# Convolution over f of the first batch: the mean is subtracted on VectorE and the constant goes into the gelu

## The chip, the cores and the metric

The kernel runs on one core of one Trainium2 chip. Its metric is the device time of one execution in microseconds (us), lower is better. Before the change the median of three runs is 3683.86 us, with 3683.42 and 3687.7 us as the lowest and the highest.

## The reference, cut to what matters

Two layers run one after the other on x of shape (4, 512, 128, 64), all in float32: four batches b, 512 time steps t, and 128 x 64 = 8192 features d = (f, h). The first layer is the one that is changed:

```python
xn = layernorm(x.reshape(b, t, d), ln_attn_g, ln_attn_b)
k, v, r = xn @ Wk, xn @ Wv, sigmoid(xn @ Wr)
states = scan over t of  s = decay * s + k * v
x = x + (r * states) @ Wo
xn = layernorm(x.reshape(b, t, d), ln_freq_g, ln_freq_b)   # statistics over all 8192 features
fo = conv over f, 3 taps, 64 x 64 channels h, of xn         # 'SAME' padding
x = x + gelu(fo + freq_b)
x = x + layernorm(causal depthwise conv over t, 3 taps, of layernorm(x))
x = x + W2 gelu(W1 x + b1) + b2                             # over h, 64 -> 256 -> 64
```

The second layer is a moving average over t plus a filter in the Fourier domain. It comes after the whole first layer and is not touched.

With rs = 1/sqrt(var + eps) and m the mean of one time step, the normalized value is x1\*rs - m\*rs. Each of these is one value per time step, so a row of 512 numbers that is the same for all features.

## The kernel before

The features lie on the partitions: a batch is 64 chunks of 128 features (two values of f, 64 of h) by 512 time steps, and the work goes in 32 pairs of chunks. A pair is a tile of 128 x 1024 float32. Each float32 matmul of the code stands in the trace as two matmul records.

For each batch b the first layer is made of stages, written as Python generators:

- `project` (J): k, v and r for all 512 steps, summed over the 32 pairs on TensorE (L412), with the weights scaled on VectorE (L359) and the statistics of the layernorm.
- `scan` (Z): the recurrence on VectorE with a few matmuls, which ends in rows for the next norm.
- `attend_and_convolve` (A): for each pair i, `attend(i)` makes x1 = x + Wo product (TensorE L534, VectorE L538) and z = x1 \* rs (VectorE L542). `convolve(i)` makes the convolution over f of pair i in PSUM, the gelu in place in PSUM (ScalarE L574), x2 = gelu + x1 (VectorE L576), the store of x2 (POOL queue, L579) and its square (ScalarE L581). `add_up` sums x2 and its square over the features with matmuls by ones (L250). The steps are staggered: step i attends pair i, convolves pair i-2 and adds up pair i-3.
- `convolve_time` (C), `open_feed` and `feed_forward` (O, F): the causal convolution over t and the feed forward.

The convolution leaves out the mean in z, and brings it in by a product of small rank. For every pair `convolve` has three groups of matmuls into the same PSUM tile `cv`: four 64 x 64 products of two constant rows of weights `cgs` with two rows `mb` (L560; one row is m\*rs, the other is ones, so that the mean and the constant from ln_freq_b and freq_b come in together); four 64 x 64 products with the neighbouring values of f (L568); and two full 128 x 128 products of the chunks themselves (L573). The constant rows are made once in `prepare`, written to DRAM (`cgd`), and read back two rows at a time: `scaled(i+2)` issues two small transfers from the SP queue (L548) and scales the taps on ScalarE (L553). Line L524 turns half of the rows of `mb` into ones.

TensorE's order is written out by hand: `in_turn` draws steps from two streams of stages by weights. For the first batch the streams are Z and A of batch 0 beside J and Z of batch 1, and after that C of batch 0 beside A of batch 1. The other engines' order comes from the scheduler. While J of batch 1 runs, its sums hold the PSUM tile `m` (`held`), so that every convolution of batch 0 uses the one tile `c`. Later the pairs take turns between `m` and `c`.

The pools matter too: the input tile `xp` has three buffers that J and A share, the weights `wk` of J have two, `cgs` three, `z` four.

Of the kernel before, what the change touches and what calls it, by code (L numbers as in the profile page):

```python
# [10 lines left out]
F32 = mybir.dt.float32  # L11
AF = mybir.ActivationFunctionType
ALU = mybir.AluOpType
# [3 lines left out]
P = 128  # L17
# [4 lines left out]
NCH = D // P  # L22
SL = 512
NS = D // SL
NPR = NCH // 2
# [55 lines left out]
def layer0(ctx, tc, dram, x, xt, vecs, wkvr, wo, wdec, wconv, fbias, w1, fb1, w2, fb2, x4):  # L81
# [4 lines left out]
    nc = tc.nc  # L86
# [9 lines left out]
    const = ctx.enter_context(tc.tile_pool(name="const", bufs=1))  # L96
# [9 lines left out]
    def two(pool, tag):  # L106
        return pool.tile([P, 2, SL], F32, tag=tag, name=tag)
# [47 lines left out]
    at_one = const.tile([P, 2], F32, name="at_one")  # L155
    nc.vector.tensor_reduce(at_one[:, 0:1], ident.rearrange("p (q k) -> p q k", k=32)[:, :, 1], mybir.AxisListType.X, ALU.add)
    nc.vector.tensor_scalar(at_one[:, 1:2], at_one[:, 0:1], -1.0, 1.0, ALU.mult, ALU.add)
    tb_all = vec[:, TB, :]
    fix = vec[:, G3 : B3 + 1, :].rearrange("p k c -> p c k")

    AHEAD = 14
    halves = [slice(0, H), slice(H, P)]

    def neighbours(q, c):

        return (c - 1, q), (c + 1, 1 - q)

    def rows_of(q, d):

        return 1 - q if d < 0 else q  # L170

    def prepare():

        both = rowp.tile([P, SL], F32, tag="rg", name="both")[:, 0:P].rearrange("p (k c) -> p k c", k=2)

        pcs = two(ps_c, "c"), two(ps_m, "m")
        for k, v in ((0, G2), (1, B2)):
            for r in range(2):
                for q in range(2):
                    j = r if q == 0 else 1 - r  # L180
                    o, src = pcs[r][:, k, 0:NCH], vec[:, v, :]
                    at = slice(2 * q + j, NCH, 4)
                    nc.tensor.matmul(
                        o[:, at], lhsT=wc_sb[:, q, 0:P], rhs=src[:, at], start=q == 0, stop=True,
                        skip_group_check=True,
                    )
                for q in range(2):
                    j = r if q == 0 else 1 - r
                    for d, n in neighbours(q, 0):
                        first, last = 2 * q + j, 2 * q + j + NCH - 4  # L190
                        first, last = first + 4 * (first + d < 0), last - 4 * (last + d >= NCH)
                        qn = (first + d) // 2 % 2
                        rs = halves[rows_of(qn, d)]
                        nc.tensor.matmul(
                            pcs[r][halves[n], k, first : last + 1 : 4], lhsT=wc_sb[rs, qn, P:],
                            rhs=vec[rs, v, first + d : last + d + 1 : 4], start=False, stop=True,
                            skip_group_check=True,
                        )
        for r in range(2):
            for q in range(2):  # L200
                at = slice(2 * q + (r if q == 0 else 1 - r), NCH, 4)
                nc.vector.tensor_scalar_mul(both[:, 0, at], pcs[r][:, 0, at], -1.0)
                nc.vector.tensor_scalar(both[:, 1, at], pcs[r][:, 1, at], fb_sb, None, ALU.add)
        pg = two(ps_c, "c")
        nc.tensor.transpose(pg[:, 0, 0:P], both.rearrange("p k c -> p (k c)"), ident)
        cgt = rowp.tile([P, SL], F32, tag="state", name="cgt")[:, 0:P]
        nc.vector.tensor_copy(cgt, pg[:, 0, 0:P])
        for k in range(2):
            nc.scalar.dma_start(cgd[:, k, :], cgt[k * NCH : (k + 1) * NCH, :])

        t012 = rowp.tile([P, SL], F32, tag="rg", name="t012")[:, 0 : 3 * NCH].rearrange("p (k c) -> p k c", k=3)
        t0, t1, t2 = t012[:, 0, :], t012[:, 1, :], t012[:, 2, :]
        nc.vector.tensor_tensor(t0, vec[:, W0, :], vec[:, B3, :], ALU.mult)
        nc.vector.tensor_tensor(t1, vec[:, W1, :], vec[:, B3, :], ALU.mult)
        nc.vector.tensor_tensor(t1, t1, t0, ALU.add)
        nc.vector.tensor_tensor(t2, vec[:, W2, :], vec[:, B3, :], ALU.mult)
        nc.vector.tensor_tensor(t2, t2, t1, ALU.add)
        nc.vector.tensor_tensor(tb_all, vec[:, TB, :], t2, ALU.add)  # L220
        for k in (W0, W1, W2):
            nc.vector.tensor_tensor(vec[:, k, :], vec[:, k, :], vec[:, G3, :], ALU.mult)
        nc.vector.tensor_scalar_mul(fix[:, :, 0], t1, -1.0)
        nc.vector.tensor_scalar_mul(fix[:, :, 1], t0, -1.0)
# [63 lines left out]
    def pair_of(row):  # L288
        return row.unsqueeze(1).to_broadcast([P, 2, SL])
# [11 lines left out]
    def c_bank():  # L301
        return two(ps_c, "c")
# [217 lines left out]
    def attend_and_convolve(b):  # L520
        rst, rs, mrs = scanned.pop(b)
        rb, mb = yield from rows(of_a, rs, mrs, "rm4" if b == 1 else "rm")

        nc.vector.tensor_scalar(mb, mb, at_one[:, 1:2], at_one[:, 0:1], ALU.mult, ALU.add)  # L524
        x1s, zs, ws, waiting = {}, {}, {}, {}

        def attend(i):
            xp = load_x(b, i)
            wo_sb = fr.tile([P, P], F32, tag="wo", name="wo_sb")
            nc.sync.dma_start(wo_sb, wo[:, i, :])  # L530
            at = two(ps_a, "a")
            for j in range(2):
                for hs in halves:
                    nc.tensor.matmul(  # L534
                        at[hs, j, :], lhsT=wo_sb[halves[j], hs], rhs=rst[halves[j], :], start=True, stop=True
                    )
            x1 = x1s[i] = fr.tile([P, 2, SL], F32, tag="x1", name="x1")
            nc.vector.tensor_tensor(x1, at, xp, ALU.add)  # L538
            z = fr.tile([P, 2, SL], F32, tag="z", name="z", bufs=4)
            for j in range(2):  # L540
                zs[2 * i + j] = z[:, j, :]
            nc.vector.tensor_tensor(z, x1, pair_of(rb), ALU.mult)  # L542

        def scaled(i):

            for j in range(2):
                at = H * (j ^ i % 2)
                nc.sync.dma_start(cgs[i % 3][at : at + 2, :], cgd[2 * i + j])  # L548
            wcs = fr.tile([P, 2, P + H], F32, tag="wcs", name="wcs")
            for j in range(2):  # L550
                c = 2 * i + j
                ws[c] = wcs[:, j, :]
                nc.scalar.mul(wcs[:, j, :], wc_sb[:, i % 2, :], vec[:, G2, c : c + 1])  # L553

        def convolve(i):
            cv = c_bank() if i % 2 or held[0] else two(ps_m, "m")
            for j in range(2):
                rs = halves[j ^ i % 2]
                for hs in halves:
                    nc.tensor.matmul(  # L560
                        cv[hs, j, :], lhsT=cgs[i % 3][rs, hs], rhs=mb[rs, :], start=True, stop=False
                    )
            for j in range(2):
                c = 2 * i + j
                for n, h in neighbours(i % 2, c):
                    if 0 <= n < NCH:
                        rs = halves[rows_of(n // 2 % 2, n - c)]
                        nc.tensor.matmul(  # L568
                            cv[halves[h], j, :], lhsT=ws[n][rs, P:], rhs=zs[n][rs, :], start=False, stop=False
                        )  # L570
            for j in range(2):
                c = 2 * i + j
                nc.tensor.matmul(cv[:, j, :], lhsT=ws[c][:, 0:P], rhs=zs[c], start=False, stop=True)  # L573
            nc.scalar.activation(cv, cv, AF.Gelu_apprx_tanh)  # L574
            x2 = two(bk, "x2")
            whole_x2 = nc.vector.tensor_tensor(x2, cv, x1s.pop(i), ALU.add)  # L576
            if i == NPR - 2:
                begin[project] = whole_x2.ins
            nc.gpsimd.dma_start(x2d[b][2 * i : 2 * i + 2].rearrange("c p t -> p c t"), x2)  # L579
            sq2 = bk.tile([P, 2, SL], F32, tag="sq", name="sq2")  # L580
            nc.scalar.activation(sq2, x2, AF.Square)  # L581
            for c in (2 * i - 2, 2 * i - 1):
                zs.pop(c, None)
                ws.pop(c, None)
            if i + 2 < NPR:
                scaled(i + 2)
            waiting[i] = x2, sq2
# [282 lines left out]
    def nothing(b):  # L870
# [5 lines left out]
    whole = {  # L876
        J: 2.0 * NPR, Z: 7 * CHAIN, A: 7.0 * NPR + 3 * CHAIN, C: 7.0 * (NPR + 2) + 3 * CHAIN, O: 4 * CHAIN,
        F: 9.0 * (NPR + 1), nothing: 1.0,
    }
# [345 lines left out]
```

## Time and profile before

| | us |
|---|---|
| median of three runs | 3683.86 |
| the profiled execution, its own time | 3685.27 |
| span of the profiled execution | 3683.5 |
| TensorE busy in the span | 3480.4 (94%) |
| VectorE busy | 2671.6 (73%) |
| ScalarE busy | 1778.1 (48%) |
| GpSimd busy | 448.4 (12%) |
| mean granted TensorE clock | 0.985 of full |

The profiled execution is 1.8 us longer than its span. Busy time of TensorE counts a matmul from its start to the modelled end, and several small matmuls in different parts of the array run at once, so 94% does not mean that the array is at its peak. What the change touches is `attend_and_convolve` of batch 0 only, whose first convolution starts at 242 us and whose last gelu starts at 515 us of the span. The stages of the other batches are not changed.

### The profile page before, as it was taken

Reading aid. Unit: us, or ns where it says so; the run is one execution under the profiler, and the core shown is the slowest. Engines: PE = TensorE matmul, PEld = TensorE weight load, DVE = VectorE, ACT = ScalarE, POOL = GpSimd, SP = SyncE. Lnnn points to the kernel's source line nnn. Section 1 sums busy time; section 2 is a strip of 40 time slices with the busy share of each in tenths; the row PEclk is TensorE's granted clock in tenths of the full one; section 3 lists DMA queues with packets and bytes.
Section 4 is the critical chain, followed back from the end, with each engine's and each line's share of the span. In section 5 each row is a group of like instructions: output and inputs, shape, how many; then the busy total and the mean of one; then the engine's idle time right before and its main releaser. Section 6 shows DMA issues by size and latency. Waiting matters only on the chain. (4 is left out here: it accounts for less than half of the span.)

```text
span 3683.5 us, 54528 instructions
## 1 busy us (share of the span) xinstructions
PE 3480.4 (94%) x20553; PEld 1372.7 (37%) x20553; DVE 2671.6 (73%) x3498; ACT 1778.1 (48%) x2331; POOL 448.4 (12%) x657
## 2 busy tenths in 40 slices
PE   8989998889999899999999989999999999999998
PEld 3433332224333223443322333333333833328433
DVE  4464469986777896677789799956677277892677
ACT  0013346556666565666656588878864200152100
POOL 0000012220111121011112121200000000001000
PEclk9999999999999999999999999999999999999999
DMA  9886647787885688888568777746668478994687
GB/s 302 284 269 211 204 164 269 255 277 264 294 288 183 237 279 280 277 289 292 172 239 284 239 238 256 238 173 218 225 194 277 154 245 293 308 290 161 209 298 261
DMA packets 427991, 910.58 MB, mean 247 GB/s; under 512 B 32976, under 2 KB 83920, under 8 KB 423632
## 3 DMA queue, kind: packets, MB, share of 16 engines
q1 hardware_dynamic: 354160, 637.18, 53.1%
q0 software_dynamic: 71680, 268.46, 20.3%
q8 instruction: 164, 2.69, 0.3%
q10 hardware_dynamic: 1888, 1.45, 0.1%
q14 instruction: 99, 0.81, 0.1%
HBM read 638.46 MB, written 268.50 MB: 246 GB/s over the span
## 5 line engine op out<-in xcount | busy, mean ns | idle before, releaser
L760 PE MATMUL p<-mid,w_sb 64*64 64x512 f32 x2048 | 549.3, 595 | 17.9 <-DVE wx L773 17.9
L760 PE MATMUL pb<-mid,w_sb 64*64 64x512 f32 x2048 | 533.2, 595 | 0.0
L750 ACT ACTIVATE mid<-m,fb_sb 128x1024 f32<-128x1024 f32 x256 | 284.8, 1113 | 93.0 <-PE m L745 91.6
L750 ACT ACTIVATE mid<-c,fb_sb 128x1024 f32<-128x1024 f32 x256 | 284.5, 1111 | 91.2 <-PE c L745 89.1
L745 PE MATMUL m<-x,w_sb 64*64 64x512 f32 x2016 | 283.3, 613 | 7.5 <-ACT ob L794 5.3
L745 PE MATMUL c<-x,w_sb 64*64 64x512 f32 x2016 | 276.9, 604 | 12.9 <-ACT mid L750 6.6
L760 PEld LDWEIGHTS p<-mid,w_sb 64*64 64x64 f32 x2048 | 153.7, 134 | 290.9 <-issue 261.0
L1071 ACT COPY two<-a 128x512 f32<-128x512 f32 x64 | 37.5, 586 | 426.3 <-PE a L1066 426.3
L412 PE MATMUL a<-xp,wx 128*128 128x512 f32 x512 | 235.2, 603 | 0.5 <-DVE me L267 0.5
L1094 PE MATMUL b<-xin,avg_sb 128*128 128x512 f32 x512 | 230.8, 593 | 3.3 <-DVE xin L1100 3.3
L1100 DVE TENSOR_TENSOR xin<-b,pm 128x512 f32<-128x512 f32 x256 | 159.0, 683 | 97.9 <-PE b L1097 82.9
L581 ACT ACTIVATE sq<-x 128x1024 f32<-128x1024 f32 x128 | 135.1, 1055 | 150.5 <-DVE x L576 150.4
L250 PE MATMUL st<-x,ones 128*32 128x512 f32 x512 | 183.9, 609 | 23.8 <-DVE x L576 23.7
L636 DVE SCALAR_TENSOR_TENSOR to<-kd,vec,to 128x511 f32<-128x511 f32 (+1 forms) x272 | 197.0, 743 | 11.5 <-ACT to L632 8.0
L713 ACT ACTIVATE kd<-kd,vec 128x512 f32<-128x512 f32 x256 | 192.7, 803 | 3.1 <-DVE kd L705 3.1
L538 DVE TENSOR_TENSOR x<-a,xp 128x1024 f32<-128x1024 f32 x128 | 156.1, 1219 | 48.1 <-PE a L534 45.5
L946 DVE COPY xf<-b 128x256 f32<-128x256 f32 x128 | 54.4, 425 | 178.9 <-PE b L1040 170.0
L636 DVE SCALAR_TENSOR_TENSOR z<-x,vec,z 128x511 f32<-128x511 f32 x240 | 175.6, 744 | 5.0 <-ACT z L632 3.6
L716 DVE TENSOR_TENSOR x<-kd,kx 128x1024 f32<-128x1024 f32 x126 | 154.0, 1223 | 33.5 <-ACT kd L713 33.5
L534 PE MATMUL a<-rst,wo_sb 64*64 64x512 f32 x1024 | 143.3, 630 | 27.4 <-DVE x L538 25.3
L773 DVE SCALAR_TENSOR_TENSOR x4t<-p,fb_sb,x 128x512 f32<-128x512 f32 x64 | 47.7, 746 | 160.0 <-PE pb L760 157.5
L704 DVE TENSOR_TENSOR kd<-kh,rm 128x1024 f32<-128x1024 f32 x128 | 155.6, 1219 | 6.8 <-ACT rm L284 4.6
(271 smaller groups left out, 6762.7 us busy)
## 6 DMA issues: line engine op xcount, KB each, us to landing
xp<-in_xt SPq DMA_DIRECT2D x256, 512.0 KB
kh<-to SPq DMA_DIRECT2D x156, 512.0 KB
x<-x POOLq DMA_DIRECT2D x128, 512.0 KB, 4.6
kx<-x SPq DMA_DIRECT2D x128, 512.0 KB
x<-ob POOLq DMA_DIRECT2D x64, 1024.0 KB, 8.1
xin<-x SPq DMA_DIRECT2D x64, 1024.0 KB
out<-xin POOLq DMA_DIRECT2D x64, 1024.0 KB, 6.3
x<-x SPq DMA_DIRECT2D x96, 512.0 KB
```

The costliest lines, as they stand in the source:

```text
L250: nc.tensor.matmul(st[32 * q : 32 * q + 32, :], lhsT=ones, rhs=src[:, j, :], start=first, stop=last,)
L412: nc.tensor.matmul(pa[:, k, :], lhsT=wq[:, j, k * P : (k + 1) * P], rhs=xp[:, j, :], start=first and j == 0, stop=last and j == 1,)
L538: nc.vector.tensor_tensor(x1, at, xp, ALU.add)
L636: tap = nc.vector.scalar_tensor_tensor(to[:, j, k:], xr[:, j, : SL - k], vec[:, w, c], to[:, j, k:], ALU.mult, ALU.add)
L704: nc.vector.tensor_tensor(d, to, pair_of(rb), ALU.mult)
L713: tc.keep_in_program_order(nc.scalar.activation(d[:, j, :], d[:, j, :], AF.Identity, bias=vec[:, B4, c], scale=vec[:, G4, c]))
L716: nc.vector.tensor_tensor(x3, d, x2, ALU.add)
L745: nc.tensor.matmul(pm[halves[j], h, :], lhsT=w1_sb[halves[h], q * H : (q + 1) * H], rhs=x3[halves[h], j, :], start=True, stop=True,)
L750: gelu = nc.scalar.activation(mid, pm, AF.Gelu_apprx_tanh, bias=fb1_sb[:, q : q + 1])
L760: nc.tensor.matmul(sums2[i][j][halves[h], :], lhsT=w2_sb[halves[j], q, :], rhs=mid[halves[j], h, :], start=q == 0, stop=q == 3,)
L1094: nc.tensor.matmul(po[j], lhsT=avg_sb[:, j, :], rhs=xin[:, j, :], start=True, stop=False)
L1100: nc.vector.tensor_tensor(by_n(xin[:, j, :]), by_n(po[j]), by_c(pm[j % 2][:, j // 2, :]), ALU.add)
```

## The change

For batch 0 alone (`whole`), the mean is subtracted from z on VectorE right after the product with rs, the four products with constant rows are left out together with the transfers of their weights, and the constant (a column of 128 values for each chunk, `cbias`, kept when `prepare` makes it) is the bias of the gelu. As the bias differs from chunk to chunk, the gelu becomes two instructions of 128 x 512 in place of one of 128 x 1024. As no product covers the whole tile any more before the neighbours' products, these start the sums themselves, with the chunk's own products after them; at the two ends, where a neighbour is missing, the own products come first. Line L524 is left out for batch 0.

```diff
@@ layer0, prepare
+    cbias = const.tile([P, NCH], F32, name="cbias")
...
+        nc.vector.tensor_copy(cbias, both[:, 1, :])
@@ attend_and_convolve
-        nc.vector.tensor_scalar(mb, mb, at_one[:, 1:2], at_one[:, 0:1], ALU.mult, ALU.add)
+        whole = b == 0
+        if not whole:
+            nc.vector.tensor_scalar(mb, mb, at_one[:, 1:2], at_one[:, 0:1], ALU.mult, ALU.add)
@@ attend
             nc.vector.tensor_tensor(z, x1, pair_of(rb), ALU.mult)
+            if whole:
+                nc.vector.tensor_tensor(z, z, pair_of(mb), ALU.subtract)
@@ scaled
-            for j in range(2):
+            for j in range(2 * (not whole)):
                 at = H * (j ^ i % 2)
                 nc.sync.dma_start(cgs[i % 3][at : at + 2, :], cgd[2 * i + j])
@@ convolve
-            for j in range(2):
+            for j in range(2 * (not whole)):
                 rs = halves[j ^ i % 2]
                 for hs in halves:
                     nc.tensor.matmul(
                         cv[hs, j, :], lhsT=cgs[i % 3][rs, hs], rhs=mb[rs, :], start=True, stop=False
                     )
+
+            def own(start):
+                for j in range(2):
+                    c = 2 * i + j
+                    nc.tensor.matmul(cv[:, j, :], lhsT=ws[c][:, 0:P], rhs=zs[c], start=start, stop=True, skip_group_check=whole)
+
+            edge = whole and i in (0, NPR - 1)
+            if edge:
+                own(True)
...
                         nc.tensor.matmul(
-                            cv[halves[h], j, :], lhsT=ws[n][rs, P:], rhs=zs[n][rs, :], start=False, stop=False
+                            cv[halves[h], j, :], lhsT=ws[n][rs, P:], rhs=zs[n][rs, :],
+                            start=whole and not edge, stop=whole, skip_group_check=whole,
                         )
-            for j in range(2):
-                c = 2 * i + j
-                nc.tensor.matmul(cv[:, j, :], lhsT=ws[c][:, 0:P], rhs=zs[c], start=False, stop=True)
-            nc.scalar.activation(cv, cv, AF.Gelu_apprx_tanh)
+            if not edge:
+                own(False)
+            if whole:
+                for j in range(2):
+                    c = slice(2 * i + j, 2 * i + j + 1)
+                    nc.scalar.activation(cv[:, j, :], cv[:, j, :], AF.Gelu_apprx_tanh, bias=cbias[:, c])
+            else:
+                nc.scalar.activation(cv, cv, AF.Gelu_apprx_tanh)
```

## The prediction, made before the changed kernel ran

> **What bounds the kernel now.** I read the busy times by stage first, then TensorE's order of time inside one pair, then what VectorE waits for, then the end of the stage.
>
> ```profile
> core 0: us, PE busy (x) PEld busy (x) DVE busy (x) ACT busy (x) POOL busy (x), PEclk, DMA share, GB/s
> 250.00:450.00 200.00, 199.88 (x976) 66.46 (x972) 95.61 (x116) 65.12 (x90) 18.25 (x25) 1.00 0.64 214
> 450.00:475.00 25.00, 24.31 (x142) 8.71 (x134) 17.38 (x20) 13.89 (x20) 2.18 (x3) 1.00 0.58 195
> 475.00:500.00 25.00, 21.73 (x114) 9.05 (x114) 11.62 (x16) 6.89 (x10) 2.79 (x4) 0.80 0.37 129
> 500.00:520.00 20.00, 18.94 (x112) 5.05 (x114) 9.39 (x9) 10.94 (x17) 3.01 (x4) 1.00 0.36 131
> 545.00:800.00 255.00, 226.29 (x1273) 58.94 (x1271) 252.66 (x280) 157.02 (x215) 68.86 (x92) 0.99 0.78 261
> ```
>
> The convolutions of batch 0 lie between 242 and 515 us. From 250 to 450 us, beside `project` of batch 1, TensorE is never idle, VectorE and ScalarE are under half, the transfers at 0.64. From 545 us on (C of batch 0 with A of batch 1) VectorE is the bound, 252.66 of 255. So time won before 545 us moves everything behind it forward; no later stage waits for a fixed moment.
>
> ```profile
> 447.91 0.21 PEld L534 LDWEIGHTS a<-rst,wo_sb 64*64 64x64 f32 x8 [0.84 <-issue]
> 448.39 0.15 PEld L560 LDWEIGHTS c<-rm,cg 64*64 64x64 f32 x4 [0.28 <-issue]
> 448.82 0.15 PEld L560 LDWEIGHTS c<-rm,cg 64*64 64x64 f32 x4 [0.28 <-issue]
> 449.25 0.15 PEld L568 LDWEIGHTS c<-z,wcs 64*64 64x64 f32 x4 [0.28 <-issue]
> 450.64 0.30 PEld L573 LDWEIGHTS c<-z,wcs 128*128 128x128 f32 x2 [0.81 <-issue]
> ```
>
> The mean duration must not be summed here: eight records of L560 at 589 ns would be 4.7 us a pair. The starts show the truth: four run at once, the two sets of four start 0.43 us apart, and L568 follows at 449.25. The constant products hold TensorE for 449.25 - 448.39 = 0.86 us a pair.
>
> The gelu begins at 272.90 in the fourth pair and at 436.22 in the 22nd: 163.32 us for 18 pairs, 9.07 us a pair. TensorE's sets make up 8.57 of that at 0.43 us each: 8 for L412, 4 for L573, and 2 for each of L250, L534, L560 and L568. The rest is the gaps between kinds of tile. So the pair is bound by TensorE's issue.
>
> **The change, part by part.**
>
> *The constant products go.* 20 pairs (the fourth to the 23rd) x 0.855 = 17.1 us on the path, if nothing else takes the place. The order listings of both kernels agree on TensorE apart from these 128 products and the ends' own products.
>
> *The subtraction comes.* 32 x 1.22 us, by the equal operation of `convolve_time` (L627, 128x1024, mean 1216 ns), 39 us in all on VectorE. In the steady stage it has a cover: VectorE is busy 95.61 of 200, and 20 more subtractions make 120 of some 183. z is first read by the convolution one step later. What stands behind it in VectorE's queue is one of the two scalings of `wk` and the x2 addition (L576), which frees PSUM tile `c`. Without cover it would cost 1.22 us a pair, more than the 0.86 won.
>
> *The gelu is split.* The new order makes the second half wait for the first, and only the first waits for TensorE, so I let both come after all products. No row has a PSUM to PSUM half with a bias. The nearest is the copy of 128x512 from PSUM at 587 ns (L284); a bias column adds 107 ns (L750 at 1112 against L574 at 1005). That gives 0.69; the upper end is 0.80, by L713 with two columns. Two of them and a hand-over are 1.45 us in place of 1.01, so `c` comes free 0.45 us later after the last product. ScalarE's total (65 of 200) covers the work. What the latency meets is this:
>
> ```profile
> 309.97 1.01 ACT L574 ACTIVATE c<-c 128x1024 f32<-128x1024 f32 x1 [1.13 <-PE c L573]
> 311.01 1.23 DVE L576 TENSOR_TENSOR x<-c,x 128x1024 f32<-128x1024 f32 x1 [3.22 <-ACT c L574]
> 313.06 0.15 PEld L560 LDWEIGHTS c<-rm,cg 64*64 64x64 f32 x4 [0.28 <-issue]
> ```
>
> Here x2 ends at 312.24 and the next convolution writes `c` at 313.06, a slack of 0.8 us, one of the shortest; most pairs have 2.5 to 3. The slack is counted from the last product to the next first one, which the change leaves alone. 0.45 fits.
>
> *Transfers go.* 64 small issues of about 0.26 us leave SP's queue. They are no load, but SP stands still for their buffer until L560 is done, and the load of `wk` is behind them:
>
> ```profile
> 370.14 0.24 SPq L548 DMA_DIRECT2D cg<-cgd  x1
> 370.43 0.37 SPq L392 DMA_DIRECT2D wk<-in_wkvr  x1
> ...
> 375.00 0.55 DVE L359 TENSOR_SCALAR wk<-wk,vec 128x192 f32<-128x192 f32 x2 [5.27 <-DMA wk<-in_wkvr]
> 375.47 1.22 DVE L576 TENSOR_TENSOR x<-c,x 128x1024 f32<-128x1024 f32 x1
> ...
> DVE wk L359 <- DMA wk<-in_wkvr: 40.2, 19, 5.3
> ```
>
> This is the weak place. VectorE's queue is in order. When `wk` lands late, as at 375.00, x2 waits though its gelu was over at 373.93. The changed order is z, scaling, subtraction, scaling, x2, so a late landing then carries 1.22 us more. In its favour the `wk` load is issued about 1 us earlier in such pairs. Two of some 20 pairs show it now. I take 2 us of new stalls in all, between 0 and 20 x 0.65 = 13.
>
> *The start.* The first three convolutions run while VectorE is nearly full of statistics, scalings and first z. They win 2.6 us on TensorE and add 3 x 1.22 = 3.7 us on VectorE. At the first end the own products need only the first z and can go ahead. I take 0, between -1.5 and 2.6. The dropped L524 (0.55 us) and the copy of `cbias` (0.15, by the small VectorE rows) have nobody waiting.
>
> *The last nine pairs* run beside the scan of batch 1.
>
> ```profile
> 476.49 1.07 PE L501 MATMUL p<-rst,qo 64*64 64x512 f32 x2 [2.18 <-DVE rst L496]
> ```
>
> Pairs 25 to 27 end in this wait for VectorE's chain to `rst`. There a pair holds x1, z, x2, L479 and L480 at 1.22, 1.22, 1.22, 0.75 and 0.68, and with the subtraction 6.3 us, while TensorE needs 5.7 to 6.7. Laying them out in the new order, `rst` comes about 1.15 us earlier than now, not 3 x 0.86, and TensorE then waits some 4 us. The other six pairs win 6 x 0.855 = 5.1. The last gelu, x2, square and sum form a plain chain, which the split lengthens by 0.45. Together 5.8, between 0 and 8.
>
> [...]
>
> Sum: 17.1 + 0 + 5.8 - 2 = 20.9, call it 21 us. It is made on the execution of 3685.27 us (span 3683.5 and 1.8 around it), 1.4 us above the median and inside the runs' spread. From the median: 3683.9 - 21 = 3663 us.
>
> **The rivals.**
>
> A, the above: TensorE's issue is the bound and stays so. For it: 199.88 of 200 busy. 3657 to 3670 us.
>
> B, half lost: late `wk` and the longer way through gelu and x2 stall every pair of the steady stage by about 0.5 us: 20 x 0.5 = 10 more. Gain 11, 3673 us. For it: 19 waits for `wk`. Against: most end well before x2's turn.
>
> C, hidden: the gain of the steady stage is eaten by input loads, which keep the old pace. Against: `xp` ends only stray waits, and 0.64 of the engines at 9.07 us a pair is 0.71 at 8.2, where 0.92 was reached in the first 150 us. 3684 us.
>
> D, slower: the tile `c` becomes the bound. If `wk` lands after the gelu in every pair, each x2 starts after scaling, subtraction and scaling, 1.5 us later than a landing alone allows; less the 0.86 won, it is 0.65 a pair. Over 23 pairs that is 15 us, and VectorE's longer chain to `rst` adds 2: 3701 us. It decides where the landing comes later than 3 us before `c` is needed (0.28 + 1.22 + 0.3 + 1.23). At 307.24 it came 5.8 us before 313.06, but at 375.00 only 1.7 us before 376.74, so the point isn't far.
>
> That the change does less than it says is excluded: the order listing has 128 products and 64 transfers fewer.
>
> **How the numbers follow.** A 0.62, B 0.16, C 0.08, D 0.14. 0.2% is 7.4 us, about what a measurement of this kernel can tell from no change. Faster by more: A and most of B, 0.77; within: C and the edge of B, 0.10; slower: D but for its mildest end, 0.13. The likeliest time is A's, 3663. The range 3652 to 3680 holds A with the bounds of its parts (17.1 + 2.6 + 8 would be 3656, and a luckier clock a little less), B, and the near edge of C.
>
> **What would show it.** Right: gelu starts of the steady pairs about 8.2 us apart in place of 9.07, TensorE still full, the last gelu of batch 0 some 21 us before 515, and the stage from 545 us moved forward as it is. The subtraction at about 1.22 us, a gelu half at 0.7. The wait for `rst` near 4 us. Wrong: TensorE idle before L568 with x2 as the releaser (B, D), longer waits for `xp` (C), or gelu halves of 0.8 us and more.

## The result, and the profile after

The changed kernel takes 3664.63 us (median of five runs, 3658.0 to 3669.1), the kernel before on the same chip 3683.42 us: a ratio of 0.9939, with 0.9925 to 0.9953 as its 95% interval, or 18.8 us less. The same pair measured once more gave 3673.19 against 3691.72 us, a ratio of 0.9955 (0.9943 to 0.9967), 18.5 us less. The forecast was 3663 us, 21 us less.

In the changed file most lines have moved: L412 is now L414, L534 is L538 (Wo product), L538 is L542 (x1), L542 is L546 (z), L568 is L583 (neighbours), the own products are L573, L574 is L592 (gelu of batch 0), L576 is L596 (x2), L496 is L498 and L501 is L503 (the scan's end). The subtraction is L548.

Busy times by stage, in the columns of the table shown for before:

```profile
core 0: us, PE busy (x) PEld busy (x) DVE busy (x) ACT busy (x) POOL busy (x), PEclk, DMA share, GB/s
250.00:400.00 150.00, 147.05 (x646) 48.52 (x639) 97.84 (x116) 58.06 (x93) 14.59 (x21) 1.00 0.70 238
450.00:475.00 25.00, 20.11 (x91) 7.03 (x84) 16.76 (x23) 10.02 (x15) 2.77 (x4) 0.75 0.39 135
475.00:500.00 25.00, 21.84 (x114) 6.54 (x118) 15.05 (x14) 14.14 (x24) 2.90 (x4) 0.98 0.45 153
520.00:775.00 255.00, 226.30 (x1279) 59.10 (x1275) 253.82 (x281) 156.85 (x215) 68.57 (x91) 1.00 0.78 261
```

TensorE is still nearly full in the steady stage (147.05 of 150), VectorE has gone from just under half to 65%, and the transfers from 0.64 to 0.70: about the same bytes in less time. The stage that now lies from 520 us on is the old one from 545 us, with VectorE full. The loss of clock, which stood at 0.80 from 475 to 500 us before, is in the second row: 0.75 from 450 to 475 us.

The timeline of the weight loads of one pair:

```profile
306.02 0.21 PEld L538 LDWEIGHTS a<-rst,wo_sb 64*64 64x64 f32 x8 [0.84 <-issue]
306.50 0.15 PEld L583 LDWEIGHTS c<-z,wcs 64*64 64x64 f32 x4 [0.28 <-issue]
306.93 0.15 PEld L583 LDWEIGHTS c<-z,wcs 64*64 64x64 f32 x4 [0.28 <-issue]
307.90 0.30 PEld L573 LDWEIGHTS c<-z,wcs 128*128 128x128 f32 x2 [0.81 <-issue]
```

The two sets of L560, which stood 0.43 us each between the Wo product and the neighbours, are gone, and nothing has taken their place. The same pair's other engines:

```profile
309.81 1.22 DVE L548 TENSOR_TENSOR z<-z,rm 128x1024 f32<-128x1024 f32 x1
309.98 1.36 ACT L592 ACTIVATE c<-c,cbias 128x512 f32<-128x512 f32 x2 [1.19 <-PE c L573]
311.37 1.22 DVE L596 TENSOR_TENSOR x<-c,x 128x1024 f32<-128x1024 f32 x1
312.63 1.06 ACT L601 ACTIVATE sq<-x 128x1024 f32<-128x1024 f32 x1 [1.29 <-DVE x L596]
```

The subtraction takes 1.22 us, the two gelus 1.36 us together, and x2 (L596) still begins as soon as the gelu is over.

How far each pair moved is read from the starts of the gelu. The steps from one pair to the next, in us (fourth pair to the 22nd, the tile `c` with all its waits in it):

| step | before | after | won |
|---|---|---|---|
| 4 to 5, 5 to 6 | 9.08, 9.28 | 8.31, 8.77 | 0.77, 0.51 |
| 6 to 7, 7 to 8 | 9.27, 9.44 | 8.42, 8.58 | 0.85, 0.86 |
| 8 to 9, 9 to 10 | 7.36, 9.08 | 6.50, 8.22 | 0.86, 0.86 |
| 10 to 11, 11 to 12 | 9.08, 9.28 | 8.22, 8.42 | 0.86, 0.86 |
| 12 to 13, 13 to 14 | 9.28, 9.43 | 8.42, 8.58 | 0.86, 0.85 |
| 14 to 15, 15 to 16 | 9.44, 7.72 | 8.58, 7.54 | 0.86, 0.18 |
| 16 to 17, 17 to 18 | 9.08, 9.08 | 8.22, 8.22 | 0.86, 0.86 |
| 18 to 19, 19 to 20 | 9.27, 9.28 | 8.42, 8.42 | 0.85, 0.86 |
| 20 to 21, 21 to 22 | 9.44, 9.43 | 8.58, 8.58 | 0.86, 0.85 |

Fifteen of 18 steps won 0.85 or 0.86 us, the two sets that are gone. The whole stretch, which I call "the stage" from here on, goes from the first Wo product of batch 0 to the ScalarE copy of its square sums at the end:

| us | before | after | difference | the two once more |
|---|---|---|---|---|
| start: first Wo product to the fourth gelu | 37.8 | 35.8 | -2.0 | 38.7 to 36.0 |
| steady: fourth to 22nd gelu | 163.3 | 149.0 | -14.3 | 163.0 to 149.6 |
| tail: 22nd gelu to the copy of the sums | 83.5 | 78.9 | -4.6 | 83.2 to 78.5 |
| the stage | 284.6 | 263.7 | -20.9 | 284.8 to 264.1 |

Of the start's 2.7 us in the second pair, 1.7 are the clock: the start of that execution of before has 3.41 us at half speed in it (236.45 to 239.86 us), the other three have none.

Right behind the stage nothing changes pace: the next stage (sums of batch 0 to sums of batch 1) is 279.6 us long in both. At the last sums of the first layer, at 2404 us in after, the changed kernel is 22.8 us ahead, and at the end of the profiled execution 17.0 (3685.27 and 3668.25). So 5.8 us are lost again in the second layer, which has the same instructions in both. In the second pair of executions the lead is 22.1 us at that place and 19.5 at the end. This is not shown to be mere spread: from these sums to the end the two executions of before take 1257.0 and 1257.2 us, the two of the changed kernel 1262.8 and 1259.8, and the ten other kernels below, all with edits in the first layer alone, 1260.7 to 1266.1. It fits that the runs won 18.8 and 18.5 us where the stage won 20.9 and 20.7. What makes the second layer longer stays open.

### The profile page after: what moved, and what is told of

It reads as the page before. It is cut to its first block, busy times and chain, and to the rows that moved or that the text cites. A ratio compares the mean times of both kernels' runs of the same rounds, so it can differ in the third digit from the quotient of the medians.

```text
span 3666.5 us, 53980 instructions
## 1 busy us (share of the span) xinstructions
PE 3458.3 (94%) x20297; PEld 1363.8 (37%) x20297; DVE 2707.6 (74%) x3530; ACT 1787.3 (49%) x2363; POOL 448.6 (12%) x657
## 3 DMA queue, kind: packets, MB, share of 16 engines
q10 hardware_dynamic: 1888, 1.45, 0.1%
## 5 line engine op out<-in xcount | busy, mean ns | idle before, releaser
L770 ACT ACTIVATE mid<-m,fb_sb 128x1024 f32<-128x1024 f32 x256 | 284.6, 1112 | 92.0 <-PE m L765 90.8
L414 PE MATMUL a<-xp,wx 128*128 128x512 f32 x512 | 235.2, 603 | 0.5 <-DVE me L269 0.5
L542 DVE TENSOR_TENSOR x<-a,xp 128x1024 f32<-128x1024 f32 x128 | 156.0, 1219 | 38.2 <-PE a L538 35.6
L538 PE MATMUL a<-rst,wo_sb 64*64 64x512 f32 x1024 | 143.3, 627 | 27.5 <-DVE x L542 25.2
```

The source lines that it names most:

```text
L414: nc.tensor.matmul(pa[:, k, :], lhsT=wq[:, j, k * P : (k + 1) * P], rhs=xp[:, j, :], start=first and j == 0, stop=last and j == 1,)
L770: gelu = nc.scalar.activation(mid, pm, AF.Gelu_apprx_tanh, bias=fb1_sb[:, q : q + 1])
```

## The experiments

### One part at a time: products, loads, subtraction, gelu

The first kernel is the changed one without the subtraction and with the old single gelu; the small loads of `cgs` are issued again (second hunk):

```diff
-            if whole:
-                nc.vector.tensor_tensor(z, z, pair_of(mb), ALU.subtract)
...
-            for j in range(2 * (not whole)):
+            for j in range(2):
...
-                    nc.scalar.activation(cv[:, j, :], cv[:, j, :], AF.Gelu_apprx_tanh, bias=cbias[:, c])
+            nc.scalar.activation(cv, cv, AF.Gelu_apprx_tanh)
```

> The kernel after, but with no subtraction and one gelu of 128x1024 without a constant: for batch 0 the constant products are left out and nothing takes their place (its mean and its constant are left out), while the small loads of their weights are still issued on SP. Measure: the stage of batch 0, from its first product with Wo to the copy of its sums, 284.6 us before the change and 263.7 after it. Theory (TensorE's issue of the constant products was the price): the stage is 257 to 261 us, the time 23 to 28 us below the kernel before. Rival S (the gain comes from SP, whose queue no longer stands still behind the small loads): the loads are still there, so the stage stays above 275 us and the time within 10 us of before.

The second is the same, but leaves the small loads out as the changed kernel does.

> As the one before (no constant products, no mean and no constant for batch 0), and the small loads of their weights left out too. Theory: within 2 us of that kernel, stage 256 to 261 us, because the loads are no work of TensorE and the loads of wk mostly have slack. Rival S: 10 us or more faster than with the loads. Both kernels bound what subtraction and split gelu cost the kernel after: by the theory 4 to 6 us of the stage, mostly at the start and on the way to rst.

The third is the kernel before with the subtraction put in beside the constant products:

```diff
             nc.vector.tensor_tensor(z, x1, pair_of(rb), ALU.mult)
+            if b == 0:
+                nc.vector.tensor_tensor(z, z, pair_of(mb), ALU.subtract)
```

> The kernel before with the subtraction of the row added behind every z of batch 0, and everything else kept (so the mean is taken away twice). It prices the 32 subtractions alone in the old stage. Theory (VectorE has room there): stage 286 to 291 us, that is 1 to 6 us longer, most of it in the first three pairs and on the way to rst; time 1 to 7 us above before. Rival D (VectorE's queue is the close second bound, since the late wk holds the subtraction and x2): at least 0.65 us a pair, stage 300 us or more, time 15 us or more above before.

The fourth is the changed kernel with one gelu of 128x1024 and no constant in it.

> The kernel after with one gelu of 128x1024 for batch 0 in place of two halves; the constant is left out. It prices the split. Theory: the split adds 0.35 us to each gelu, which only the last chain of the stage and a few pairs that wait for the tile c feel: stage 261.5 to 263.5 us, 0.2 to 2 us shorter than in the kernel after, time within 5 us of it. Rival B (the longer way through gelu and x2 stalls every pair): stage 258 us or less.

| us | run (median) | ratio, 95% interval | start | steady, per pair | tail | stage |
|---|---|---|---|---|---|---|
| products out only | 3670.15 | 0.9933 (0.9907 to 0.9959) | 36.8 | 8.323 | 74.2 | 260.9 |
| products and loads out | 3668.01 | 0.9936 (0.9912 to 0.9960) | 35.9 | 8.291 | 75.0 | 260.2 |
| subtraction beside products | 3694.02 | 1.0008 (0.9995 to 1.0021) | 40.7 | 9.053 | 80.8 | 284.5 |
| changed, one gelu | 3674.32 | 0.9951 (0.9934 to 0.9968) | 35.2 | 8.339 | 81.0 | 266.4 |

The kernel before took 3689.22 us on this chip.

- The products alone bring the whole steady gain: 8.32 us a pair against 8.28 in the changed kernel, which does the subtraction and the split gelu on top. In the steady stage both additions are free.
- The loads count for nothing: 260.9 and 260.2. The rival that SP's queue made the gain is out.
- The subtraction and the split gelu were to cost the changed kernel 4 to 6 us of the stage. It is 2.8 and 3.5 us longer than these two, and 3.4 us of that are two lengths of slow clock more in its tail (table further down), so together they cost little. The run of the first, 19.1 us below before, missed the 23 to 28 that were expected of it.
- The subtraction alone leaves the steady period where it was (9.053 against 9.073 and 9.053 in the two executions of before). Its stage, 284.5, came below what was expected, 286 to 291, but its tail drew less slow clock (3.4 us at half speed against 10.2 in before, worth some 3.4 us). The first three pairs did pay: 40.7 against 38.7 in the execution of before whose start has the same 3.41 us at half speed in it, and 37.8 in the one that has none. The run, 4.8 us above before, is not clear of the noise.
- The fourth missed in the wrong direction: 266.4 where 261.5 to 263.5 was expected, though it has less work. The steady stage is unmoved, and the excess is all in the tail: 81.0 us, against 78.9 in the changed kernel, which has more to do. That needs another cause, and the granted clock is one: over the tail its mean is 0.95, 0.95, 0.98 and 0.89 in these four, 0.94 in before and 0.91 in after. The runs on the tail below settle this.

### How far VectorE's cover reaches

```diff
-                nc.vector.tensor_tensor(z, z, pair_of(mb), ALU.subtract)
+                for _ in range(3):
+                    nc.vector.tensor_tensor(z, z, pair_of(mb), ALU.subtract)
```

> The changed kernel with batch 0's subtraction done three times in a row (the mean is taken away three times). VectorE then has 2 x 1.22 = 2.44 us more a pair: from some 5.4 us of 8.28 in the steady stage to 7.9, still below the period. Theory (the subtraction is hidden as long as VectorE has room, but its queue is in order, so some of x2 comes late): the period rises from 8.28 to between 8.4 and 9.2 us, and the first three pairs and those beside the end of the scan, where VectorE is nearly full, take 3 x 2.4 = 7 us more each; the stage 275 to 295 us against 263.7. Rival (the place in the queue costs the whole length, wherever VectorE stands): 8.28 + 2.44 = 10.7 us a pair, the stage over 310 us.

Busy times in the steady stage of this kernel, fourth to 22nd gelu:

```profile
276.70:432.40 155.70, 152.91 (x641) 49.41 (x640) 138.94 (x147) 57.30 (x91) 13.46 (x19) 0.99 0.66 221
```

The waits of TensorE's matmuls in it (in all, times, longest; L584 and L597 are L583 and L596, moved by a line):

```profile
PE c L584 <- DVE x L597: 2.7, 2, 2.1
```

The run takes 3700.06 us (1.0027, 1.0019 to 1.0035, of before), so with three subtractions the change would have lost. The pair is 8.65 us long in place of 8.28: of 2.44 us more on VectorE 0.37 shows, though VectorE is now busy 138.94 of 155.70. Where VectorE had no room the price is higher: the first three pairs take 43.6 us, 7.8 more, for 3 x 2.44 = 7.3 us of added work. Their mean clock is 0.92 in place of 1.00, two lengths of 3.41 us at half speed, which is 3.4 of the 7.8; so the work itself cost between 4.4 and 7.8, as the slow clock may come of the added waits. The tail is 94.1, 15.2 more where some 7 were expected, with 3.4 again in slower clock. The stage, 293.3, is inside the 275 to 295 of the theory, and the rival (10.7 us a pair) is out.

### The same edit where VectorE is the bound

```diff
-        whole = b == 0
+        whole = b < 2
```

> The changed kernel with the same edit in batch 1's convolution over f too (constant products out, subtraction and two gelus with a constant in). There the convolution of batch 0 over h and w runs beside it, and VectorE was busy 252.66 of 255 us with TensorE at 226. Theory (the change pays only where TensorE is the bound and VectorE has room): 32 subtractions x 1.22 us = 39 us come on an engine with no room, so this stage (from the square sums of batch 0 to those of batch 1, 279.6 us in the changed kernel) gets 25 to 40 us longer, and the run takes 3690 to 3710 us. Rival (the products cost TensorE time wherever they stand): the stage gets shorter once more, by some 20 us, to about 260.

Busy times of the stage from the square sums of batch 0 to those of batch 1, in this kernel:

```profile
492.10:820.10 328.00, 256.30 (x1142) 66.26 (x1142) 294.35 (x312) 173.93 (x252) 70.64 (x93) 0.85 0.62 211
```

The longest of TensorE's waits in it:

```profile
PE m L583 <- DVE z L548: 25.3, 11, 3.8
PE c L583 <- DVE z L548: 17.3, 10, 2.4
```

The row of busy times of the changed kernel for its own stage:

```profile
497.30:776.80 279.50, 247.36 (x1401) 67.41 (x1400) 269.13 (x298) 165.03 (x225) 72.25 (x97) 0.99 0.76 254
```

The run takes 3726.85 us, 1.0099 (1.0080 to 1.0117) of before: slower, as the theory said, though by more, as 3690 to 3710 us and a stage 25 to 40 us longer were expected. The stage grew by 48 us. The products' TensorE time is gone here too, but TensorE now stands 42.6 us waiting for the subtracted z (21 times), a wait that the changed kernel doesn't have, and its mean clock is 0.85 in place of 0.99. Counted to the square sums of batch 2, which takes in what is shifted out of the stage, it is 993.0 us against 930.4, 62.6 more. 39 us of it would be the 32 subtractions; what the low clock and the waits took of the rest no run here separates.

The counterpart leaves batch 1's constant products out and puts nothing in their place:

```diff
-            for j in range(2 * (not whole)):
+            bare = whole or b == 1
+            for j in range(2 * (not bare)):
...
```

> The changed kernel with batch 1's constant products over f left out and nothing put in their place: batch 1's mean and constant are left out of the computation. It takes 128 products of one row off TensorE in the stage where VectorE is busy 252.66 of 255 us. Theory (there TensorE is not the bound): the stage between the square sums of the two batches stays at 279.6 us within 3. Rival (each pair of constant products costs 0.855 us wherever it stands): 32 x 0.855 = 27 us shorter, 252.

The run takes 3668.68 us, 0.9937 (0.9915 to 0.9959) of before, no different from the changed kernel's 0.9939. The marker that was forecast missed: the stage is 270.7 us, 8.9 shorter, neither "within 3" nor 27. But from the square sums of batch 0 to those of batch 2 it is 930.9 us against 930.4. The 8.9 us are given back in the stage behind, because the convolution over t was only postponed. Over both, 128 products fewer on TensorE are worth nothing where VectorE is the bound.

### The subtraction on GpSimd at the end of the scan

```diff
-                nc.vector.tensor_tensor(z, z, pair_of(mb), ALU.subtract)
+                engine = nc.gpsimd if 24 <= i < 29 else nc.vector
+                engine.tensor_tensor(z, z, pair_of(mb), ALU.subtract)
```

> The changed kernel with the subtraction of five pairs (25th to 29th), the ones beside the end of batch 1's scan, on GpSimd in place of VectorE. Theory (there VectorE's chain to rst is the bound and the subtraction stands in it): rst comes 1.5 to 3 us earlier after the 22nd gelu than in the changed kernel, and TensorE's wait for rst, 3.12 us, goes below 2.2; what the stage wins is the same size as long as the granted clock stays. Rival (GpSimd's 128x1024 addition is slow and z comes late): the products wait for GpSimd, 2 us or more a pair, and the stage is 5 to 10 us longer.

VectorE around the end of the scan's chain in this kernel:

```profile
441.64 0.75 DVE L481 SCALAR_TENSOR_TENSOR wx<-rm,gw,p 128x512 f32<-128x512 f32 x1 [1.12 <-PE p L477]
...
447.29 0.75 DVE L481 SCALAR_TENSOR_TENSOR wx<-rm,gw,p 128x512 f32<-128x512 f32 x1 [0.77 <-PE p L477]
...
452.01 1.21 DVE L542 TENSOR_TENSOR x<-a,xp 128x1024 f32<-128x1024 f32 x1
453.14 1.21 DVE L496 TENSOR_TENSOR_SCAN state<-decb,wx 128x512 f32<-128x512 f32 x1
454.27 1.19 DVE L546 TENSOR_TENSOR z<-x,rm 128x1024 f32<-128x1024 f32 x1
455.39 0.68 DVE L498 TENSOR_TENSOR rst<-rg,state 128x512 f32<-128x512 f32 x1
```

Both theories fell. `rst` comes 36.24 us after the 22nd gelu against 36.69, 0.45 earlier and not 1.5 to 3; TensorE's wait is 3.03 us against 3.12; nothing waits long for GpSimd's 2.35 us (the median of five) either, and the run is 3667.08 us (0.9937, 0.9921 to 0.9953), the same as the changed kernel. VectorE's chain has gaps of its own that wait for TensorE's small products (L477), and the last links stand behind x1 and z of the next pair. Without any subtraction (the first two experiments) `rst` comes 0.6 us earlier after the 24th gelu (21.37 and 21.38 against 21.97). So the subtraction delays `rst` by about half a microsecond.

### The tail and the clock

Repeats of both kernels, unaltered:

> The changed kernel once more, unaltered. Theory (the last pairs' time is set by when TensorE is put to half speed, which is luck of one execution): the steady period is 8.28 us within 0.03 again, but the tail (22nd gelu to the copy of the square sums, 78.9 us at a mean clock of 0.91) differs by 2 us or more between two executions, in step with its granted clock. Rival (the clock loss belongs to this kernel's order): the tail is 78.9 within 0.5 and its clock 0.91 again.

> The kernel before once more, unaltered: steady period 9.07 us within 0.03. By the same theory its tail (83.5 us at a mean clock of 0.94) is 80 to 86 us, in step with the clock; by the rival 83.5 within 0.5.

The tails came out as 78.5 (after) and 83.2 (before), within 0.4 us of the first executions and with the same mean clocks, 0.91 and 0.94. As written, the theory of luck missed. The granted clock in half-microsecond slices shows why the value is so stable. But for slices in which it changes, it is only ever 1.00 or 0.50, and the stretches at 0.50 in the tail are these:

| kernel | start of each stretch and its length, us | sum | tail |
|---|---|---|---|
| before | 478.14: 3.41, 488.38: 6.83 | 10.24 | 83.5 |
| before again | 475.38: 3.41, 485.62: 6.83 | 10.24 | 83.2 |
| after | 455.68: 6.83, 469.34: 6.82 | 13.65 | 78.9 |
| after again | 456.10: 6.83, 469.75: 6.83 | 13.66 | 78.5 |
| products out only | 459.91: 6.83 | 6.83 | 74.2 |
| products and loads out | 455.02: 6.83 | 6.83 | 75.0 |
| subtraction beside products | 489.10: 3.42 | 3.42 | 80.8 |
| changed, one gelu | 455.07: 6.82, 468.72: 10.24 | 17.06 | 81.0 |
| edit in both batches | 463.17: 6.83 | 6.83 | 75.2 |
| batch 1's products out | 453.20: 6.83, 466.86: 6.83 | 13.65 | 78.7 |
| subtraction on GpSimd | 456.82: 3.41, 467.06: 6.83 | 10.24 | 76.6 |
| subtraction three times | 465.89: 6.83, 489.78: 10.24, 513.67: 3.41 | 20.48 | 94.1 |

All are one, two or three times 3.41 us. The changed kernel has one such length more than before, and at the granted 0.50 each costs TensorE half of itself, 1.7 us, an estimate. The one-gelu kernel has one more still, which is 1.7 of the 2.1 us by which its tail is longer than that of the changed kernel. The kernels "batch 1's products out" and "edit in both batches" have the same instructions as after in batch 0: the first drew the same lot as after, the second has two lengths less and a tail 3.7 us shorter. So luck there is, only the repeats didn't show it.

The first stretch sits at the wait for `rst`. To try that, the wait is filled:

```diff
+        for _ in range(3 if b < 2 else 0):
+            nc.tensor.matmul(pq[0:S, :], lhsT=ident[0:S, 0:S], rhs=decb[0:S, :], start=True, stop=True)
```

> The changed kernel with three more matmuls of 64x64 weights and 512 columns ahead of the product that waits for rst, for the scans of both batches; they write a bank that this product overwrites. They keep TensorE at work for most of its 3.1 us wait. Theory (the wait puts TensorE to half speed for the next few us): the half-speed stretch right behind this product goes, and the tail is 2 to 4 us shorter than 78.9 (70 to 72 us are what is left of it when all the clock loss is taken out). Rival (the clock is not set by that gap): the stretch stays, the tail is the same or 1 us longer.

TensorE's timeline at this place, in the changed kernel:

```profile
455.82 1.97 PE L503 MATMUL p<-rst,qo 64*64 64x512 f32 x2 [3.12 <-DVE rst L498]
457.71 1.06 PE L252 MATMUL st<-x,ones 128*32 128x512 f32 x1
```

and with the filler (L504):

```profile
452.69 1.02 PE L504 MATMUL p<-decb,ident 64*64 64x512 f32 x2
454.11 1.07 PE L505 MATMUL p<-rst,qo 64*64 64x512 f32 x2 [0.41 <-DVE rst L498]
455.11 0.62 PE L252 MATMUL st<-x,ones 128*32 128x512 f32 x1
```

The product for `rst` takes 1.97 us at half speed and 1.07 at full, the sums behind it 1.06 and 0.62. Busy times in steps of 4 us round this product, in the changed kernel:

```profile
451.82:455.82 4.00, 0.88 (x4) 0.05 (x2) 4.00 (x5) 3.47 (x6) 0.00 (x0) 0.98 0.47 157
455.82:459.82 4.00, 4.00 (x14) 0.72 (x18) 3.02 (x4) 0.00 (x0) 0.00 (x0) 0.50 0.43 129
459.82:463.82 4.00, 4.00 (x18) 1.04 (x15) 2.82 (x3) 0.83 (x2) 0.72 (x1) 0.66 0.44 151
```

and with the filler:

```profile
450.11:454.11 4.00, 3.60 (x9) 0.77 (x7) 4.00 (x5) 3.48 (x6) 0.00 (x0) 1.00 0.47 155
454.11:458.11 4.00, 4.00 (x27) 0.99 (x28) 3.88 (x5) 0.91 (x1) 0.64 (x1) 1.00 0.48 135
458.11:462.11 4.00, 4.00 (x24) 2.56 (x28) 3.72 (x6) 2.17 (x5) 0.09 (x1) 1.00 0.80 267
```

The stretch is gone, and the tail is 75.7 us, 3.2 shorter, as the theory said; all of it lies between `rst` and the copy of the sums (39.0 us against 42.2). By itself this one execution would not do, since the kernel with the edit in both batches has no first stretch either. But the next kernel, which has the same filler, shows none at this place, and without a filler eight of twelve executions do (last section): the wait for `rst` brings the first stretch. The run as a whole is 3672.45 us (0.9950, 0.9936 to 0.9964), beside 3673.19 for the changed kernel on the same chip, no gain that can be told: in the profiled execution the steady stage was 3.4 us longer, with three waits of the neighbours' products for x2 (3.7 us) in place of one (0.8). That the filler causes these isn't shown.

> As the last one, with two more such matmuls ahead of the first spreading of the row statistics in the norm of both batches, where TensorE waits for GpSimd. Theory: the half-speed stretches beside the spreading go as well; with both, the tail is up to 7 us shorter than 78.9, and the run up to 10 us faster than the changed kernel. Rival: the new matmuls stand in TensorE's queue ahead of work that others wait for, and win nothing.

The edit of this last kernel, on top of the filler just shown:

```diff
-    def rows(bank, a, b, names):
+    def rows(bank, a, b, names, fill=0):
...
+            for _ in range(fill if k == 0 else 0):
+                nc.tensor.matmul(pb[0:S, :], lhsT=ident[0:S, 0:S], rhs=decb[0:S, :], start=True, stop=True)
...
```

Nothing was won, as the rival said. The second stretch did not go: it is 10.24 us long from 470.53 on, the tail 78.0 us and the run 3676.37 (0.9962, 0.9950 to 0.9975). Busy times in the 3.41 us ahead of it and in the stretch itself:

```profile
467.12:470.53 3.41, 3.41 (x26) 2.20 (x27) 2.12 (x6) 1.30 (x2) 0.82 (x2) 1.00 0.56 165
470.53:480.77 10.24, 9.56 (x29) 3.63 (x28) 4.47 (x5) 2.44 (x4) 1.24 (x2) 0.50 0.23 74
```

TensorE counts as busy throughout ahead of the stretch, so it is not the wait for GpSimd that puts the clock down here. But for 1.74 of the 3.41 us nothing runs except one-column matmuls (L511 and L512 of the changed kernel, 16 records of a column each); the last section comes back to them. No version here beats the changed kernel.

## Why the prediction was right, point by point

**The constant products.** Right to the hundredth: 0.855 us a pair was read from the issue times, and 15 of 18 steps won 0.85 or 0.86. The products alone give it all, and the same kind of products are worth nothing where VectorE is the bound (930.9 us without them against 930.4, to the square sums of batch 2). That TensorE's issue bounds the pair is shown from both sides.

**The subtraction.** Right in duration (1.22 us) and in its cover in the steady stage: with it or without it 8.28 to 8.34 us a pair, and two more of them show only 0.37 of 2.44.

**The gelu.** 0.69 us a half and 1.45 for two were forecast, 1.36 for two came. One gelu in place of two leaves the period where it was.

**New stalls: 2 us forecast, some 1 to 2 came, at the place named.** Three steps fell short of 0.855, by 0.09, 0.35 and 0.68 us, 1.1 in all; in the second pair of executions it was 2.0. The worst is at the 16th pair. The timeline of the changed kernel there:

```profile
363.12 0.55 DVE L361 TENSOR_SCALAR wk<-wk,vec 128x192 f32<-128x192 f32 x2 [2.81 <-DMA wk<-in_wkvr]
363.59 1.22 DVE L596 TENSOR_TENSOR x<-c,x 128x1024 f32<-128x1024 f32 x1
364.86 1.09 PE L583 MATMUL c<-z,wcs 64*64 64x512 f32 x8 [0.81 <-DVE x L596]
```

`wk` lands late, its scaling and then x2 follow at once, and the products that overwrite `c` wait for x2. The undisturbed step there is 6.50; with the subtraction it was between 7.5 and 8.7 in eight executions, without it 6.53 and 6.85. But in this pair the subtraction does not stand between the scaling and x2, as the prediction had it; it was over before the load landed. How it makes this pair later all the same was not tried.

**Rivals B, C and D.** None came to be. The late landing stops one or two pairs, not each; D's threshold was a landing later than 3 us before `c` is needed, and the landing of 363.12 came less than that before 364.05, when TensorE stood ready (364.86 less its wait of 0.81), which fits the threshold; one landing doesn't prove it. `xp` stops TensorE once, for 0.3 us. (The transfers' share in the first 150 us, given as 0.92 under C, is 0.91 in the trace, which changes nothing.)

**The start: 0 forecast, 2.0 came,** inside its bounds of -1.5 to 2.6. The step that was off is the 3 x 1.22 us on VectorE, which was set against the gain in full: with the products gone 35.8 us with the subtraction and 35.9 without it. It does cost when the products stay, 40.7 against 38.7 at the same clock. Why the two differ stays open.

**The last nine pairs: 5.8 forecast.** With two of the 20 steady pairs the tail was to win 7.5 us; it won 4.6. (The one tile `c` that the description above gives to all of batch 0 holds for the first 24 pairs; from the 25th on `m` and `c` take turns, in both kernels, with the first gelu in `m` at 460.35 before and 440.03 after.) Split up:

| part of the tail | forecast | measured |
|---|---|---|
| 22nd to 24th gelu | 1.7 | 1.73 |
| 24th gelu to `rst` | 1.15 | 1.11 |
| `rst` to the copy of the sums | 4.65 | 1.75 |

`rst` came as forecast to 0.04 us, though VectorE's total was not the whole reason, as the kernel with GpSimd shows. TensorE's wait for it grew from 2.18 to 3.12 us (4 forecast). The last gelu to the copy of the sums grew by 0.57 us (0.45 forecast). What is missing lies behind `rst`, and the clock explains 1.7 of 2.9; 1.2 us are not assigned.

**The clock.** This is the step that failed. The sum adds nothing for the clock, as if the loss that before has already (0.80 from 475 to 500 us) stayed as it is. It grew: the tail has 10.24 us at half speed before and 13.65 after, in both pairs of executions, one length of 3.41 us more and so some 1.7 us less gain, an estimate from the granted 0.50. The waits for `rst` ahead of these stretches are 2.18 and 3.12 us. It was in part a lot: with the same instructions in batch 0 the kernel with the edit in both batches had 6.83 us at half speed, less than before.

**The sum.** 20.9 forecast for the stage and 20.9 measured (20.7 the second time), as a start that was better by 2.0, stalls better by 0.9 and a tail worse by 2.9 cancel. Of the steps the products carry it; that the sum agrees so closely is luck. The run's 18.8 and 18.5 us are some 2 below the forecast. The prediction let everything behind the stage move forward as it is, and the second layer, 5.8 and 2.6 us longer after the change in the two pairs of profiled executions, did not.

## What to carry to other kernels

Read the cost of small matmuls that share the array from their starts (here 0.43 us a set of four), not from their durations (589 ns each), and take the stage's own bound before taking work from one engine to another: the same exchange made its stage 20.9 us shorter where TensorE was full, and the two stages that it reached 62.6 longer where VectorE was. Before costing work at nothing on the engine that takes it over, see how many microseconds of its queue stand ahead of the operation that frees the bound engine's buffer. Where a change makes the bound engine wait a little longer, look at the granted clock behind it: here the wait went from 2.18 to 3.12 us and the half-speed time of the tail from 10.24 to 13.65. A few filler products bridged one such wait here, with 0.41 us of it left and no half-speed stretch right behind it, but the run as a whole gained nothing that can be told.

## What the runs showed of the hardware

The half-speed stretches begin on a grid of 3.413 us: all 24 of after, from 165.55 to 3660.80 us, lie on one within 0.01 us, and so do all 24 of before, from 167.53 to 3676.43. In after four of them begin at 199.68, 213.34, 455.68 and 469.34 us, and 455.68 - 199.68 = 256.00 = 75 x 3.413. In before two begin at 201.66 and 478.14, 81 lengths apart. The 12 executions of the table above, which are all that have no filler, are laid out by how much of the wait for `rst` falls into one length of the grid: with 1.66 us of idle time or less in the fullest length (three executions) the clock stayed; with 2.18 us or more (seven) the next length was at half speed; 1.76 us went both ways (before: down, products out only: not). In these twelve the border so lies between 1.66 and 2.18 us, about half of 3.41 us. A second length followed in all four executions in which the wait reached 0.14 to 0.81 us into the first slow one, and none in two of the other three with 2.18 us or more, in which it ended sooner. By this the 3.12 us wait puts the clock down at most positions on the grid and the 2.18 us wait at fewer, an estimate from these twelve; where an execution falls on the grid seems to move its time by a few microseconds, the size of the effects studied here (a tail of 75.2 us with 6.83 us at half speed, and of 78.9 with 13.65, for the same instructions in batch 0).

Idle time is not all of it. The lengths that hold the one-column matmuls tell nothing by their idle time: 0 to 1.37 us in the eleven after which the clock went down, 0 to 1.10 in the twelve after which it stayed. Counted together with the time in which nothing but one-column matmuls ran, it is 1.74 to 2.35 us in the eleven and 0.07 to 1.80 in the twelve. The same sum fits both stretches: of the 171 lengths at full speed that begin between 440 and 492 us in all 14 executions, the 22 with half speed behind them have 1.74 us or more of it, the 149 others at most 1.80. (Further on, where two-column matmuls come in, one length with 2.01 us kept the clock.) So one-column matmuls look as if they counted as idle; that is read from the traces, and no run tried it by an edit.
